# Order of the first work: one chunk's norm first, one cell's weights at the head of the load queue, small products among the first tiles

## The chip, the cores and the metric

The kernel runs on one core of one Trainium2 chip. The metric is device time in microseconds (us) of one launch, the median of three runs. Five engines work side by side, each through its own instructions in program order: TensorE (PE; its weight loads are shown as PEld), VectorE (DVE), ScalarE (ACT), GpSimd (POOL) and SyncE (SP), which issues most of the DMAs. [...]

## The reference, cut to what matters

There are 3327 nodes with 64 features and one adjacency matrix `adj`, 3327 x 3327 in float32. Four residual layers follow each other; each is `x = x + layer(relu(layernorm(x)))`. Layer 0 is two gated graph cells with a relu behind each:

```
def _ggc(x, adj, W, wih, whh, bih, bhh):
    m = adj @ (x @ W)
    gi = m @ wih.T + bih
    gh = x @ whh.T + bhh
    r = sigmoid(i_r + h_r);  z = sigmoid(i_z + h_z)
    n = tanh(i_n + r * h_n)
    return (1.0 - z) * n + z * x
```

where `i_*` and `h_*` are thirds of `gi` and `gh`. The other layers are a product with weights made from the ranks of each row's nonzeros, three products with the squared adjacency, and two products with tanh. That makes eight products of the adjacency with a 64-wide matrix, one behind the other, called k = 0 to 7 in the kernel. The change concerns what happens before and during k = 0.

## The kernel before, in words

**Tiling.** The nodes are padded to 3328, which is 2 halves (`s`) of 13 blocks of 128. The blocks fall into four chunks, 3, 3, 3 and 4 blocks, and the chunks into two groups: group 0 is chunks 0 and 1, group 1 chunks 2 and 3. A tile of the transposed adjacency is one block of 128 source nodes (26 of them) by the target columns of one group: 768 KB for group 0, 896 KB for group 1. A unit of work `(k, c, t)` (`propagate`, L579, matmuls at L607) multiplies the features of the tile's source block with the tile's columns of chunk c, and adds into a bank of PSUM. At 384 columns in float32 a unit is 4 records of L607 in the trace.

**Stages.** `alone(0, 0, ...)` makes k = 0 for group 0 over all 26 tiles. Then `joint(1, 0, ...)` makes k = 0 for group 1, and, from the same tiles, k = 1, whose sources are the results of k = 0; further joint stages follow in the same manner. Within a stage the sources are taken chunk by chunk, so that the tiles of chunk 0 come first. `sweep=2` means that the last two tiles are used first for chunk 0's columns and then for chunk 1's, so that chunk 0 ends earlier.

**Counting.** Along with k = 0 every tile also counts its nonzeros for a later layer: a mask is made on DVE (L466, two pieces for each tile) and multiplied on PE (L542, 4 records). `lag` says by how many tiles the count follows the product. It also sets how many counts are left behind the stage's last product.

**Queues.** There are 20 buffers for tiles (`NBUF`), of which three are kept back and some hold masks. `run()` writes the load of a tile (L405, on SP) as soon as a buffer is free in program order, up to 44 units ahead; on the chip SP then waits for the buffer's last reader. SP's DMAs are taken in order.

**Tasks.** Everything beside the products is a generator in `tasks`. It writes some instructions and yields a number; `spend` (L374) subtracts an estimated product time of each unit from all these numbers (0.86 us for 512 columns) and continues a generator whose number has run out. So the order in which an engine sees its instructions is fixed when the program is built, by these numbers. What lies between two of a generator's steps is lost above the number: it continues at the next unit's end. `finish(c)` runs a generator to its end at once; `propagate` does it where the features of a chunk (`y[k][cs]`) don't exist yet (L597).

**The beginning.** `before_0(c)` (L931) is the first norm of chunk c, in four pieces: sum, mean and difference (L834 to L836); squares, their sum and scaling (L841 to L843); the power -1/2 on POOL (L845); the multiplication that writes the features (L849). After it, and after a yield of 12 to 21, come the transposes of the features (L791 on PE, L793 on ACT). The list at L1036 continues each chunk three times, so that three pieces of all four chunks are written before anything of the fourth. The first unit then finds no features and finishes chunk 0: L849, and its transposes, ahead of the first product. `more_constants` (L238) clears buffers on POOL, loads the first cell's weights into `stage` (`load_cell(0)`, two DMAs on SP behind the first 17 tiles), spreads them (`unfold_cell`, L162), multiplies W1 into the input gates (`fold_cell`, L175 and L181), and computes the third hidden gate of each chunk (`ahead_of_cell`, L201 and L202), which needs only the norm's transposed features. It does the same for the second cell later, loads more weights, and folds those of layer 2 (`fold_hops`).

**After k = 0.** When the last unit of a chunk is written, `after_0` starts: the sums go from PSUM to SBUF on ACT and DVE (L824, L825), the gates are formed (L876 on PE, L881 on ACT), DVE and ACT combine them (L886 to L908), and the result is transposed back (L774, L944). These are the sources of k = 1.

Of the kernel before, what the change touches and what calls it, by code (L numbers as in the profile page):

```python
# [87 lines left out]
def sources_of(*chunks):  # L88
    return [s * NB + b for c in chunks for s in range(2) for b in range(*CH[c])]


def upper(n):
    return slice(n * D, (n + 1) * D)
# [3 lines left out]
def kernel(  # L97
# [9 lines left out]
    nc = tc.nc  # L107
# [18 lines left out]
    stage = const.tile([P, 7 * D + NBIAS], F32, name="stage")  # L126
# [24 lines left out]
    def load_cell(cell):  # L151
        nc.sync.dma_start(out=stage[upper(0), :7 * D].rearrange("p (w f) -> p w f", f=D),
                          in_=weights[:, (W1, W2)[cell]:(W1, W2)[cell] + 7])
        if cell == 0:
            nc.sync.dma_start(out=stage[upper(0), 7 * D:], in_=bias_cols)

    def unfold_cell(cell):

        n = 3 * D + (NBIAS if cell == 0 else 0)
        i, ps = take()  # L160
        for h in range(2):
            nc.tensor.matmul(ps[upper(h), :n], ident[:, :D], stage[:, 4 * D:4 * D + n], start=True, stop=True)  # L162
        v = ps[:, :3 * D].rearrange("p (g f) -> p g f", f=D)
        for h in range(2):
            nc.vector.tensor_copy(cells[upper(1 - h), cell, h, 0:3], v[upper(1 - h)])
        if cell == 0:
            nc.vector.tensor_copy(bcol, ps[:, 3 * D:n])
        give(i)

    def fold_cell(cell):  # L170

        i, ps = take()
        for n in range(2):
            for h in range(2):
                nc.tensor.matmul(ps[upper(h), upper(n)], stage[:, :D], ident[:, :D], start=True, stop=True)  # L175
        tr = work.tile([P, P], F32, name="t2")
        nc.scalar.copy(tr, ps[:, :P])
        give(i)
        yield 1.0
        i, ps = take()  # L180
        mm(ps[:, :3 * D], tr, stage[:, D:4 * D])  # L181
        v = ps[:, :3 * D].rearrange("p (g f) -> p g f", f=D)
        for h in range(2):
            nc.vector.tensor_copy(cells[upper(h), cell, h, 0:2], v[upper(h), 0:2])
            nc.vector.tensor_copy(cells[upper(h), cell, h, 3], v[upper(h), 2])
        give(i)
# [49 lines left out]
        yield from product(1, 2)  # L236

    def more_constants():  # L238
        nc.gpsimd.memset(stage, 0.0)
        nc.gpsimd.memset(cells, 0.0)  # L240
        for c in range(NC):
            for h in range(2):
                nc.gpsimd.memset(both[c][upper(h), h], 0.0)
        nc.gpsimd.memset(bd, 0.0)
        yield 5.0
        load_cell(0)
        yield 20.0
        unfold_cell(0)
        yield 1.0

        full = work.tile([P, P], BF16, name="t2")
        nc.gpsimd.memset(full, -TWO7)
        nc.gpsimd.affine_select(out=tri, in_=full, pattern=[[-1, P]], compare_op=ALU.is_gt, fill=0.0,
                                base=0, channel_multiplier=1)
        nc.gpsimd.affine_select(out=tri, in_=tri, pattern=[[-1, P]], compare_op=ALU.not_equal, fill=TWO7 * TWO7,
                                base=0, channel_multiplier=1)
        nc.gpsimd.memset(tri[:, P - 1:P], 0.0)
        nc.gpsimd.memset(bitsb, BITS)
        nc.gpsimd.memset(lasty, 0.0)
        wide = work.tile([P, P], F32, name="t2")  # L260
        nc.gpsimd.memset(wide, 0.0)

        for i, (bi, bh) in enumerate(((BI1, BH1), (BI2, BH2))):
            nc.vector.tensor_add(bsum[:, i], bcol[:, bi:bi + 2], bcol[:, bh:bh + 2])

        nc.vector.tensor_scalar(wide[0:D], wide[0:D], bcol[0:D, BL1:BL1 + 1], None, op0=ALU.add)
        yield 3.0
        i, ps = take()
        mm(ps[:, :D], wide, ident[:, :D])
        nc.vector.tensor_copy(brow[:, 3], ps[:, :D])  # L270
        give(i)
        yield 1.0
        yield from fold_cell(0)
        for c in range(NC):
            yield 1.0
            ahead_of_cell(c)
        yield 50.0
        load_cell(1)
        yield 20.0
        unfold_cell(1)  # L280
        yield from fold_cell(1)
        yield 30.0
        for h in range(2):
            nc.sync.dma_start(out=bd[upper(h), :, upper(h)], in_=weights[:, WL1:WL3])
            for i in range(2):
                nc.sync.dma_start(out=w3[upper(h), :, i], in_=weights[:, WL3 + (h + i) % 2:NW:2])
        yield 5.0
        nc.sync.dma_start(
            out=brow[:, 0:3],
            in_=bass.AP(tensor=bias_rows.tensor, offset=bias_rows.offset, ap=[[0, P], [D, 3], [1, D]]),  # L290
        )
        yield 22.0
        yield from fold_hops()
# [5 lines left out]
    def width(c):  # L299
        return blocks(c) * P  # L300

    def mm(out, lhsT, rhs, start=True, stop=True):


        for h in range(2):
            hs = slice(h * D, (h + 1) * D)
            nc.tensor.matmul(out[hs], lhsT[:, hs], rhs, start=start, stop=stop)  # L307
# [8 lines left out]
    def take(sums=False, either=True):  # L316


        either = either and not sums
        pool = idle_sums if sums else idle_temps  # L320
        if either and idle_sums and (not pool or released[idle_sums[0]] < released[pool[0]]):
            pool = idle_sums
        for c in list(tasks):
            if not pool and c not in running:
                advance(c)
        i = pool.popleft()
        return i, banks[i]

    def give(i):
        released[i] = max(released) + 1  # L330
        (idle_sums if i < 4 else idle_temps).append(i)
# [21 lines left out]
    def advance(c):  # L353
        running.add(c)
        try:
            tasks[c][1] = next(tasks[c][0])
        except StopIteration:
            del tasks[c]
        running.discard(c)

    def begin(c, task):
        finish(c)
        tasks[c] = [task, 0.0]
        advance(c)

    def finish(c):
        while c in tasks:
            advance(c)

    def later_task(us, task):  # L370
        yield us
        yield from task
# [185 lines left out]
    def last_sources(g):  # L558

        w = sum(width(c) for c in GROUPS[g])  # L560
        w0 = CH[GROUPS[g][0]][0] * P
        room = Mask(w)
        v = room.view.rearrange("p s w -> p (s w)").bitcast(F32)
        nc.gpsimd.memset(v, 0.0)  # L564
        yield 4.0
        rows = adjT.rearrange("(q p) (s n) -> q p s n", p=P, s=2)
        for s in range(2):
            nc.sync.dma_start(out=v[s * D:s * D + NQ], in_=rows[:, P - 1, s, w0:w0 + w])
        yield 12.0
        nc.vector.tensor_scalar(v, v, 0.0, 129.0 * TWO7, op0=ALU.not_equal, op1=ALU.mult)  # L570
        for c in GROUPS[g]:
            finish(("count", c))
        yield 1.0
        nc.vector.scalar_tensor_tensor(v, totals[g], -TWO7, v, op0=ALU.mult, op1=ALU.add)
        yield 1.5
        nc.scalar.activation(lastw[g], v, AF.Relu, bias=bitsb)
        room.free()
# [61 lines left out]
    def alone(g, k, sweep, lag=None, parts=False):  # L639
        tiles = [Tile(q, g, KIND[k] == SQUARED) for q in sources_of(*range(NC))]  # L640
        counting = Counting(g, lag)
        chunks = (GROUPS[g][0], *PARTS) if parts else GROUPS[g]
        for t in tiles[:NQ - sweep]:
            for c in chunks:
                put(k, c, t)
            if lag is not None:
                counting.add(t)
        for c in chunks:
            for t in tiles[NQ - sweep:]:
                put(k, c, t)  # L650
                if lag is not None and c == GROUPS[g][0]:
                    counting.add(t)
        counting.rest()
# [277 lines left out]
    def before_0(c):  # L931
        h = nodes(c)
        yield from layernorm_relu(h, c)
        y[0][c] = h
        yield 12.0 + 3.0 * c
        transpose_to_features(h, c)

    def after_0(c, acc):
# [84 lines left out]
    after[:] = [after_0, after_1, after_2, after_3, after_4, after_5, after_6, after_7]  # L1023


    alone(0, 0, sweep=2, lag=5)
    joint(1, 0, sweep=6, later=4, keep=3, lag=2)
    joint(0, 1, sweep=4, later=20, keep=0)
    joint(1, 2, sweep=6, later=6, keep=1)
# [3 lines left out]
    joint(1, 6, sweep=8, later=4, keep=4)  # L1033
    alone(0, 7, sweep=6, parts=True)

    for c in (0, 0, 1, 0, 1, 2, 1, 2, 3, 2, 3, 3):  # L1036
        if c in tasks:
            advance(c)
        else:
            begin(c, before_0(c))  # L1040
    begin(NC, more_constants())
    begin(NC + 1, later_task(130.0, last_sources(0)))
    begin(NC + 2, later_task(155.0, last_sources(1)))
    run()
# [41 lines left out]
```

## Time and profile before

| | us |
|---|---|
| median of 3 runs | 706.61 |
| lowest and highest | 705.86, 706.64 |
| span of the profiled execution, first to last instruction | 703.7 |
| PE busy in the span | 679.8 |
| first instruction of PE | 14.92 |
| first product (L607) | 16.26 |
| last product of chunk 0 in `alone(0, 0)`, last tile | 61.00 |
| last product of chunk 1 in it | 65.41 |
| steady part of `joint(1, 0)` begins | 80.31 |

The profile gives the span and no other time of the profiled execution. The median is 2.9 us longer than that span, which holds what lies around the instructions and the difference between two executions. A row of the timeline gives start, duration from the first start to the last end of merged instructions, engine, line, operation, operands, their number, and in brackets the idle time ahead of it with what ended it. "Idle" on an engine counts only where that engine is what the others wait for.

### The profile page before, as it was taken

To read this page: it belongs to the slowest core of one execution; us is meant where nothing else is said; L and a number is where in the kernel's file an instruction comes from. 1 tells how busy PE (TensorE), PEld (TensorE's weight loads), DVE (VectorE), ACT (ScalarE), POOL (GpSimd) and SP (SyncE) were. 2 spreads that over 40 slices of the span, in tenths; PEclk is the share of its full clock that TensorE was granted. 3 is DMA by queue.
4 is the path that set the end of the run, shared out by engine and by line. 5 is a ranking of instruction groups with operands and counts; after the bars stand their busy time and mean duration, and the time that the engine had idled before them with its cause. 6 is when DMAs were issued, how large, how long until landed. Compare 5 with 4: busy or idle time off the path is not lost.

```text
span 703.7 us, 12628 instructions
## 1 busy us (share of the span) xinstructions
PE 679.8 (97%) x5100; PEld 372.9 (53%) x5100; DVE 350.1 (50%) x746; ACT 271.8 (39%) x422; POOL 80.0 (11%) x114
## 2 busy tenths in 40 slices
PE   1999999999999999999999999999999999999997
PEld 1454666643556787677444444333344444344586
DVE  7556835643997889847523105425271565005101
ACT  1014100122146888888998206832166600000101
POOL 4300000002284233111100000000000000000000
PEclk9999999999999999999999999999999999999999
DMA  9999996089686952683799649973998399927991
GB/s 344 401 385 404 406 405 241 2 314 398 209 279 253 371 177 76 246 297 96 265 390 343 245 151 409 405 276 100 398 366 271 107 391 406 406 81 276 402 403 45
DMA packets 68549, 201.31 MB, mean 286 GB/s; under 512 B 7228, under 2 KB 8228, under 8 KB 68492
## 3 DMA queue, kind: packets, MB, share of 16 engines
q1 hardware_dynamic: 65596, 199.46, 75.9%
q8 instruction: 40, 0.66, 0.4%
q10 hardware_dynamic: 720, 0.85, 0.3%
q0 software_dynamic: 2176, 0.20, 0.2%
q14 instruction: 17, 0.14, 0.1%
HBM read 199.45 MB, written 0.85 MB: 285 GB/s over the span
## 4 chain that ended last, share of the span: by engine, by line
PE 91%; DVE 7%; issue 0%; ACT 0%; DMA 0%; POOL 0%; ACTq 0%; DVEq 0%; POOLq 0%
PE sum L607 77%; PE temp L307 5%; PE temp L542 2%; PE temp L876 2%; PE sum L307 1%; DVE adj L466 1%; PE temp L774 1%; PE sum L876 1%; DVE e L521 1%; DVE st L842 1%; DVE adj L901 1%; DVE t L836 1%; DVE y L841 0%; DVE st L834 0%; DMA xs<-in_x 0%
## 5 line engine op out<-in xcount | busy, mean ns | idle before, releaser
L607 PE MATMUL sum<-adj,y 128*64 128x384 f32 (+3 forms) x3016 | 534.5, 502 | 0.7 <-DVE y L849 0.6
L607 PEld LDWEIGHTS sum<-adj,y 128*64 128x64 f32 x3016 | 243.5, 137 | 237.3 <-issue 212.4
L440 ACT ACTIVATE adj<-adj 128x768 f32<-128x768 f32 (+1 forms) x176 | 144.2, 893 | 45.8 <-PE sum L607 21.9
L466 DVE TENSOR_SCALAR adj<-adj 128x768 bf16<-128x768 f32 (+3 forms) x208 | 114.0, 597 | 39.8 <-PE temp L542 31.8
L824 ACT COPY both<-sum 64x384 f32<-64x384 f32 (+3 forms) x17 | 8.1, 478 | 192.6 <-PE sum L607 191.4
L607 PE MATMUL sum<-e,both 128*64 128x384 bf16 (+1 forms) x624 | 78.5, 339 | 0.5 <-DVE e L521 0.5
L523 ACT ACTIVATE e<-temp,bitsb 128x384 int16<-128x384 f32 (+1 forms) x117 | 66.0, 605 | 15.1 <-PE temp L307 9.9
L825 DVE COPY both<-sum 64x384 f32<-64x384 f32 (+3 forms) x17 | 9.6, 569 | 110.5 <-ACT both L824 110.5
L307 PE MATMUL temp<-adj,tri 128*64 128x384 bf16 (+1 forms) x332 | 56.8, 341 | 0.5 <-DVE e L521 0.2
L442 DVE TENSOR_TENSOR adj<-adj 128x768 f32<-128x768 f32 (+1 forms) x32 | 30.6, 1005 | 52.1 <-DMA adj<-in_adjT 33.4
L845 POOL TENSOR_TENSOR st<-st,mhalf 128x6 f32<-128x6 f32 (+1 forms) x16 | 24.0, 1498 | 283.2 <-DVE st L843 279.5
L607 PEld LDWEIGHTS <-both 128*64 128x64 bf16 x624 | 46.6, 110 | 15.5 <-issue 2.2
L307 PEld LDWEIGHTS <-tri 128*64 128x64 bf16 x416 | 33.5, 110 | 15.3 <-issue 7.1
L521 DVE TENSOR_SCALAR e<-temp 128x384 int16<-128x384 f32 (+1 forms) x49 | 30.1, 617 | 21.1 <-ACT e L523 10.5
L471 POOL DMA_DIRECT2D adj<-totals x52 | 31.5, 607 | 51.2 <-PE temp L307 40.9
L803 DVE STREAM_TRANSPOSE both<-y 32x96 f32<-32x96 f32 (+1 forms) x128 | 35.6, 278 | 2.9
L542 PE MATMUL temp<-adj,behind 128*64 128x384 bf16 x208 | 30.3, 339 | 0.9 <-DVE adj L466 0.7
L819 DVE STREAM_TRANSPOSE y<-t 32x96 f32<-32x96 f32 (+1 forms) x64 | 17.8, 278 | 24.9 <-ACT t L810 24.0
L542 PEld LDWEIGHTS <-behind 128*64 128x64 bf16 x208 | 17.0, 110 | 17.6 <-issue 15.9
L755 DVE COPY t<-sum 128x384 f32<-128x384 f32 x6 | 3.3, 555 | 35.3 <-PE sum L607 35.3
L564 POOL MEMSET adj<- 128x768 f32 (+1 forms) x2 | 1.9, 950 | 145.3 <-PE sum L607 145.3
L523 ACT ACTIVATE e<-sum,bitsb 128x384 int16<-128x384 f32 (+1 forms) x28 | 16.6, 598 | 2.5 <-PE sum L307 2.1
(132 smaller groups left out, 327.8 us busy)
## 6 DMA issues: line engine op xcount, KB each, us to landing
adj<-in_adjT SPq DMA_DIRECT2D x130, 768.0 KB, 8.5
adj<-in_adjT SPq DMA_DIRECT2D x104, 896.0 KB, 12.3
xs<-in_x SPq DMA_DIRECT2D x1, 640.0 KB
adj<-totals POOLq DMA_DIRECT2D x26, 3.0 KB, 5.1
adj<-totals POOLq DMA_DIRECT2D x26, 3.5 KB, 3.0
out<-xs ACTq DMA_DIRECT2D x2, 192.0 KB
out<-xs ACTq DMA_DIRECT2D x1, 256.0 KB
stage<-in_weights SPq DMA_DIRECT2D x2, 112.0 KB, 13.1
```

The source lines that it names most:

```text
L307: nc.tensor.matmul(out[hs], lhsT[:, hs], rhs, start=start, stop=stop)
L440: nc.scalar.activation(sq, v, AF.Square)
L442: nc.vector.tensor_tensor(sq, v, v, ALU.mult)
L466: nc.vector.tensor_scalar(t.mask.view[:rows, half], t.view()[:rows, half], 0.0, None, op0=ALU.not_equal)
L471: nc.gpsimd.dma_start(out=t.mask.view[P - 1:P], in_=totals[t.g][t.q:t.q + D + 1:D, :])
L521: nc.vector.tensor_scalar(wide[:, s], ps[:, :w], BITS, 0.0, op0=ALU.add, op1=ALU.max)
L523: nc.scalar.activation(wide[:, s], ps[:, :w], AF.Relu, bias=bitsb)
L542: nc.tensor.matmul(counts[c][1][s * D:(s + 1) * D, :w], behind[:, NQ - 1 - t.q:NQ - 1 - t.q + D], t.mask.view[:, s, t.cols(c)], start=firs ...
L607: nc.tensor.matmul(acc[h][1][h * D:(h + 1) * D, :w], yq[h], rhs[h], start=first and n == 0, stop=last and n == len(terms) - 1)
L803: nc.vector.transpose(to[at:at + 32, :, q], h[q * 32:(q + 1) * 32, :, s, f * 32:(f + 1) * 32])
L845: nc.gpsimd.tensor_tensor(st[:, 3, :n], st[:, 2, :n], mhalf[:, :n], ALU.pow)
L876: nc.tensor.matmul(ps[upper(1 - s), :w], cells[:, cell, s, g, :], both[c][:, s], start=True, stop=True)
```

## The change

The cleared `stage` and the first cell's two loads are written ahead of everything else of the tasks, so that SP has them ahead of the first tile. Chunk 0's norm is written to its end, with two thirds of chunk 1's beside it; chunks 2 and 3 begin among the first units. The transposes of a chunk come 2.5 after its norm rather than 12 to 21. The first cell's spreading comes after 4.5 rather than 25, so the folding and the third gates move forward too, with 4 rather than 1 between the four gates. The second cell's load and what follows it is counted from there, with 47 rather than 50. The count of k = 0 in group 0 follows the product by 3 tiles rather than 5.

```diff
     def more_constants():
-        nc.gpsimd.memset(stage, 0.0)
         nc.gpsimd.memset(cells, 0.0)
...
         nc.gpsimd.memset(bd, 0.0)
-        yield 5.0
-        load_cell(0)
-        yield 20.0
+        yield 4.5
         unfold_cell(0)
         yield 1.0
...
         give(i)
-        yield 1.0
+        yield 1.5
         yield from fold_cell(0)
         for c in range(NC):
-            yield 1.0
+            yield 4.0
             ahead_of_cell(c)
-        yield 50.0
+        yield 47.0
         load_cell(1)
...
         yield from layernorm_relu(h, c)
         y[0][c] = h
-        yield 12.0 + 3.0 * c
+        yield 2.5
         transpose_to_features(h, c)
...
-    alone(0, 0, sweep=2, lag=5)
+    alone(0, 0, sweep=2, lag=3)
...
-    for c in (0, 0, 1, 0, 1, 2, 1, 2, 3, 2, 3, 3):
+    nc.gpsimd.memset(stage, 0.0)
+    load_cell(0)
+    for c in (0, 0, 0, 1, 0, 1, 1):
         if c in tasks:
             advance(c)
         else:
             begin(c, before_0(c))
     begin(NC, more_constants())
+    begin(2, later_task(4.0, before_0(2)))
+    begin(3, later_task(10.0, before_0(3)))
     begin(NC + 1, later_task(130.0, last_sources(0)))
```

## The prediction

> **What bounds the kernel now.** I read the page's busy times first, then TensorE's (PE's) waits by stretch, the timeline of the beginning, the loads' landings, and the timeline where the first stage ends.
>
> ```profile
> PE 679.8 (97%) x5100; PEld 372.9 (53%) x5100; DVE 350.1 (50%) x746; ACT 271.8 (39%) x422; POOL 80.0 (11%) x114
> ```
>
> 703.7 - 679.8 leaves PE 24 us without work. The waits of PE from 0 to 20 us and from 60 to 82 us:
>
> ```profile
> PE temp L791 <- DVE y L849: 14.9, 1, 14.9
> ...
> PE temp L542 <- DVE adj L466: 0.7, 2, 0.5
> ```
>
> So 14.9 us lie ahead of its first instruction. From 20 to 60 and from 82 to 165 there are no waits; the rest of the span shows under 4 us in all. Whatever PE gains early and doesn't give back is therefore a gain of the whole. The timeline of the beginning (start, duration):
>
> ```profile
> 1.75 24.40 SPq L405 DMA_DIRECT2D adj<-in_adjT  x17
> 5.86 0.55 DVE L834 TENSOR_REDUCE st<-xs 128x6 f32<-128x384 f32 x1
> 6.04 1.34 POOL L845 TENSOR_TENSOR st<-st,mhalf 128x6 f32<-128x6 f32 x1 [4.07 <-DVE st L843]
> ...
> 14.31 1.49 DVE L849 SCALAR_TENSOR_TENSOR y<-t,st 128x384 f32<-128x384 f32 x3
> 14.92 1.55 PE L791 MATMUL temp<-ident,y 128*64 128x128 f32 x12 [14.92 <-DVE y L849]
> 16.26 9.41 PE L607 MATMUL sum<-adj,y 128*64 128x384 f32 x48
> ```
>
> Chunk 0's power is done at 7.38, but its multiplication stands on DVE behind the other chunks' norms until 14.31. The second limit is seen only in the landings. Two loads, each asked alone:
>
> ```profile
> L405 SPq DMA_DIRECT2D adj<-in_adjT x1: 602/602/602, 2.4 to 2.4; - x1
> DMA to landing us min/median/max: 7.4/7.4/7.4
> ...
> L405 SPq DMA_DIRECT2D adj<-in_adjT x1: 1721/1721/1721, 45.6 to 45.6; - x1
> DMA to landing us min/median/max: 15.3/15.3/15.3
> ```
>
> The first is the second tile (t1): it lands at 9.8. The other is the 27th issue, the first tile of group 1: it lands at 60.9, the next at 63.1 (47.4 + 15.7). Group 1's tiles thus come 2.2 to 2.3 apart (896 KB at about 400 GB/s), and group 0's last tile, t25, landed at about 60.9 - 2.25 = 58.65. In between the tiles land 1.95 apart. The windows show DMA full (share 1.00 to 1.05, 400 GB/s) from 4 to 112 us. And PE uses that last tile at 61.00:
>
> ```profile
> 61.00 0.81 PE L607 MATMUL sum<-adj,y 128*64 128x384 f32 x4
> 61.64 0.49 PE L542 MATMUL temp<-adj,behind 128*64 128x384 bf16 x4
> 61.97 1.02 PE L201 MATMUL sum<-both,cells 128*64 128x512 f32 x4
> ```
>
> So PE starts 7 us behind the stream and is only 2.35 us behind it when the stage ends. A start 6 us earlier runs into the loads.
>
> **What the skill says.** "DMA: Bandwidth & Descriptors", Queues, rings and completion order: each of the 16 DMA engines consumes a ring's descriptors in ring order. So loads written first on SP are paid by every tile behind. The trace agrees in order (9.8, 25.5, 31.4, 45.0, 60.9). Its Specifications give a ceiling of 435 GB/s; the trace's 400 to 409 is near it, so an earlier PE brings no faster loads. "TensorE: Matmul & The Clock Gate", Part 1: PE runs at half rate for its first 3.4 us or so of work. Here weight loads come 0.64 apart until 19.3 and 0.32 later: 4.4 us at half rate, a loss of 2.4 (x48 should take 7.74 rather than 9.41, and the transposes 0.82 rather than 1.55). That loss stays, wherever PE starts.
>
> **The change part by part.**
>
> *Norm order.* Chunk 0's L849 now stands behind chunk 1's L834 to L836 only (end about 7.2), so the power's end at 7.38 decides: + 0.05, + 0.55 for L849, + 0.1 to PE = 8.1. The transposes no longer stand ahead of the first product. Chunks 2 and 3 need the same 3.1 to 3.9 us of DVE each, now between masks; DVE stood idle for 5.6 us ahead of 26.03 and, but for short pieces, half of each 4 us up to 44 (2.06 busy). Their features are used from tile 12 (landing 31.4) and 18 (45.0). Hidden.
>
> *Weights ahead of the stream.* SP waits for the clearing of stage: POOL is free at 1.98, + 0.48 (L239's row) = 2.5; then two issues of 0.6 (the rows show 0.61 and 0.60 where the ring isn't full, 1.72 where it was) = 3.75 for tile 0 rather than 1.75. The 832 KB of x keep DMA busy until about 4.7 (299 GB/s from 2 to 4, 377 from 4 to 6), and the weights follow; first bytes come about 1.3 after an issue. So the hole is 0 to 0.5; I take 0.3. The weights cost 0.3 in bytes, and the window that held them before, 36 to 40, moved 336 rather than 400 GB/s, 0.64 more. That 0.94 is paid before t0 now, before t17 till now: t0 lands at 7.85 + 0.94 + 0.3 = 9.1, but t25 only 0.3 later, at 58.95. If SP were slow (1.72 each), 1.5 later; if no hole, 58.65.
>
> *PE up to the last tile.* Before: 61.00 - 14.92 = 46.1 of unbroken work. Added ahead of it: chunk 3's third gate 0.86, and two counts of 0.33, since lag 3 leaves three behind rather than five. 46.1 + 0.86 + 0.66 = 47.6; from 9.1 this gives 56.7, which is 2.2 ahead of t25. So the load decides: about 59.0, against 61.00. Gain 2.0. PE has 2.2 to spare, and this covers the moved transposes (0.66 to 0.87 each), the spreading (0.34), the folding (0.67) and the other gates: all of them counted in 46.1, moved between tiles that come 1.95 apart and take 1.61 (8 records 1.29, count 0.33).
>
> *Behind the last tile.* From 61.00 to 80.31 were 19.3. Gone: the gate 0.86, two counts 0.66. Of PE's 0.73 of waits for masks half should go: DVE was without a pause from 66.8 to 81.3, and with lag 3 the masks of the last two tiles (4 pieces of 0.55) come ahead of it; PE also comes 0.66 earlier: - 0.35. New: chunk 0's gates need L824 and L825 (0.3 + 0.47 + 0.03 + 0.56 = 1.36 after the last product), and count and product in between are 0.98, without the 0.86: + 0.4. Sum 19.3 - 0.86 - 0.66 - 0.35 + 0.4 = 17.85; 59.0 + 17.85 = 76.8 against 80.3. Gain 3.5.
>
> *POOL.* The clearing (0.95 + 5.17 + 0.53) and constants (2.2) now run from about 10.8 to 19.7, with the powers of chunks 2 and 3 behind; the spreading's copies need `cells` at about 18 (cleared at 11.8), the gates need `both` from about 26. Hidden by at least 6.
>
> *Buffers.* The third gates hold two half buffers some 30 us longer: one tile, 1.95 us of lead. SP ran 12.6 us ahead of landing where it was shortest in this stage. Nothing.
>
> *Later.* The yields up to the second cell's load sum to 74 rather than 85, so this load, its spreading (DVE 1.7 us, from 149.56) and the seven small loads (4.6 us of SP from 188.68) and the folding at 223 come 11 to 14 us earlier in the order. SP issued the second weights at 104.89, they landed at 116.2 and were used at 146.95; now about 132: still covered. The copies move from chunk 3's gates to chunk 2's; PE waits for nothing there. Without that cover 1.7; I take 0, with 0.5 to either side. From 112 us on DMA has holes (4 GB/s from 116 to 120) because buffers are full, so PE's shift passes on.
>
> The span goes from 703.7 to 700.2; the median lies 2.9 above the span, as in before: 706.6 - 3.5 = 703.1 us. A change within 0.2% (1.4 us) can't be told from none.
>
> **Rivals.**
>
> *The early start is kept whole.* If the stream has more slack than I read (the landing of t25 is from its neighbours), PE gains 14.92 - 9.1 = 5.8, plus little behind: about 700.6. For it: PE is 97% busy. Against: 58.65 and full DMA.
>
> *The stream begins late.* If the two loads cost what the ring-full issue did, or the 52-byte rows of the biases stall engines, t25 slips by 2.1 to 4.9 and eats the gain: 705.2 to 708.0, say 706. For it: 336 GB/s where they ran. Against: that dip was 0.64.
>
> *Slower.* The clearing of stage stands behind the norm's powers on POOL. SP would wait until about 11.3, tile 0 would be issued at 12.5, 8.8 us past the 3.75 above; then 703.1 + 8.8 = 712. It decides from a delay of 4.9 on, a first tile issued after 8.7. Against: the clearing is written ahead of the norms, and POOL has a pause from 1.98 to 6.04.
>
> *DVE holds the gates.* If the DVE chain behind chunk 1's last product doesn't shorten and new waits replace the 1.2 counted, the gain is the 2.0 of the load: 704.5. This is the upper end of my likeliest case, not a case apart.
>
> **How the numbers follow.** Load-bound gain 0.70, with its own range 702.0 to 704.6 (t25 between 58.65 and 59.5, the part behind between 0 and 2.2, later 0.5); whole start 0.08; late stream 0.14; slower 0.08. The range 701.0 to 705.3 takes the first, half of the second and a little of the third, 0.8. Faster: 0.70 + 0.08 + 0.01 = 0.79; same 0.13; slower 0.08.
>
> **What would show it.** The first product at about 9, without transposes ahead. PE's waits for adj loads, none till now, about 2 us in all, in the last third of the stage. The last tile's chunk-0 product at 58.7 to 59.5. No wait above 0.5 behind it beyond those for L825 and masks; steady products from about 76.8. A first tile issued after 5, or t25 later than 60, makes the prediction wrong on the slow side; a t25 used before 58 on the fast side.

## The result and the profile after

| | before | after |
|---|---|---|
| median, us (20 runs each) | 706.60 | 707.08 |
| lowest and highest | 705.50, 707.44 | 705.30, 709.48 |
| span of the profiled execution | 703.7 | 705.0 |
| first product of PE | 16.26 | 9.18 |
| last product of chunk 0, last tile (t25) | 61.00 | 58.92 |

The ratio of after to before is 1.0005, with a 95% interval of 0.9998 to 1.0012: no difference that can be measured. The likeliest forecast, 703.1, and the whole range, 701.0 to 705.3, lie below it. Lines in the changed kernel are three lower (L607 is now L604, L466 is L463, L307 is L304, L849 is L846).

The page's busy times of after:

```profile
PE 681.6 (97%) x5100; PEld 375.3 (53%) x5100; DVE 349.6 (50%) x746; ACT 272.1 (39%) x422; POOL 75.2 (11%) x114
```

PE's work is the same in number and is busy 1.8 us longer. Now its waits by stretch: the first line is from 0 to 20 us, the next two from 20 to 60, the fourth from 60 to 82, the last from 165 to 240 (total, times, longest):

```profile
PE sum L604 <- DVE st L839: 9.2, 1, 9.2
PE temp L539 <- DVE adj L463: 1.3, 3, 0.7
PE sum L604 <- DMA adj<-in_adjT: 0.3, 1, 0.3
...
PE temp L539 <- DVE adj L463: 1.4, 3, 1.0
...
PE sum L604 <- DVE brow L232: 2.8, 1, 2.8
```

The 14.9 ahead of the first instruction has become 9.2. (The row names L839; what PE needs is L846 below, written 7.52 to 8.08, and the first tile.) The last line is new: before has no wait for L232 anywhere. The beginning in the timeline of after (start, duration):

```profile
2.42 0.57 SPq L152 DMA_DIRECT2D stage<-in_weights  x1
3.04 0.59 SPq L155 DMA_DIRECT2D stage<-in_bias_cols  x1
...
3.67 11.65 SPq L402 DMA_DIRECT2D adj<-in_adjT  x11
...
7.52 0.56 DVE L846 SCALAR_TENSOR_TENSOR y<-t,st 128x384 f32<-128x384 f32 x1 [0.21 <-POOL st L842]
...
9.18 4.62 PE L604 MATMUL sum<-adj,y 128*64 128x384 f32 x16 [9.18 <-DVE st L839]
```

The first tile is issued at 3.67 and the features stand at 8.08; PE starts 1.1 later, with the tile: at the same place e1's trace, below, names the load, at 8.99. The end of the first stage:

```profile
58.92 0.87 PE L604 MATMUL sum<-adj,y 128*64 128x384 f32 x4 [0.27 <-DMA adj<-in_adjT]
```

The start and the use of the last tile came about as forecast. To find where the gain went, I followed one thing through both traces: the start of ACT's copy that takes a chunk's sums from PSUM (L821, before L824), and further on a power of a norm on POOL (L842, before L845). The table gives after's time less before's, in us, in one trace of each; the first row is where before has the event. Traces taken from one and the same order of instructions already differ by 0.5 (e8 below, up to 212 us), so smaller shifts mean nothing.

| | 66.3 | 172.1 | 212.4 | 235.2 | 278.3 | end |
|---|---|---|---|---|---|---|
| after | -2.5 | -3.7 | +2.2 | +1.0 | +0.9 | +1.4 |

The gain of 3.7 us is there at 172 us and gone, with 2.2 more, at 212. In between lies the new wait. PE there, in the timeline:

```profile
199.12 0.82 PE L224 MATMUL temp<-ident,brow 128*64 128x128 f32 x12
...
201.31 0.34 PE L304 MATMUL sum<-bd,t 128*64 128x64 f32 x4
...
206.79 0.68 PE L604 MATMUL sum<-e,both 128*64 128x384 bf16 x6 [2.82 <-DVE brow L232]
...
208.17 2.82 PE L604 MATMUL sum<-adj,y 128*64 128x384 f32 x8
```

And DVE:

```profile
202.73 3.88 DVE L463 TENSOR_SCALAR adj<-adj 127x768 bf16<-127x768 f32 x5
206.53 0.20 DVE L232 COPY brow<-sum 128x64 f32<-128x64 f32 x1
```

L224 is the beginning of `fold_hops`, the folding of layer 2's weights. Its next product, at 201.31, is written to `sum`: `take()` lends whichever bank of PSUM was released longest ago, and here that is one of the four banks in which the products of the adjacency accumulate. The next user of this bank is the product at 206.79. It has to wait until L232, a copy of 0.2 us, has emptied the bank; and this copy stands on DVE behind five mask pieces. In the kernel before, the same two steps stood elsewhere:

```profile
225.20 0.28 PE L307 MATMUL temp<-bd,t 128*64 128x64 f32 x2
...
226.58 0.22 DVE L232 COPY brow<-temp 128x64 f32<-128x64 f32 x1
```

There the folding began at 222.9, its product went to a `temp` bank, no mask pieces stood ahead of the copy, and nobody waited for it. After the wait PE is slow too. The windows of after (us, busy time and count of PE, PEld, DVE, ACT, POOL, granted clock, DMA share, GB/s):

```profile
204.00:206.00 2.00, 0.00 (x0) 0.00 (x0) 2.00 (x3) 0.90 (x2) 2.00 (x4) 1.00 0.90 286
206.00:208.00 2.00, 1.21 (x14) 1.07 (x15) 2.00 (x6) 0.17 (x1) 2.00 (x4) 0.86 0.53 166
208.00:210.00 2.00, 2.00 (x10) 1.00 (x8) 2.00 (x5) 1.15 (x3) 1.56 (x3) 0.50 0.05 12
210.00:212.00 2.00, 2.00 (x18) 1.33 (x16) 0.56 (x2) 0.00 (x0) 1.26 (x3) 0.79 0.03 5
```

The granted clock falls to 0.50: 2 x (0.14 + 0.50 + 0.21) = 1.7 us of PE's time are lost by this estimate, and the eight records of L604 at 208.17 take 2.82 us. The 20 executions agree with it: the five with a mean granted clock of 1.000 took 705.30 to 705.85, the fifteen with 0.996 to 0.998 took 706.73 or more, and their medians differ by 1.6. "TensorE: Matmul & The Clock Gate" in the Trainium skill, Part 1, says that PE drops to half rate after an idle window of about 3.4 us and needs about as long of work to come back. The trace agrees in kind, but here a pause of 2.8, shorter than that window, was enough.

### The profile page after: what moved, and what is told of

Its sections match the earlier page's. It is cut to its first block, busy times and chain, and to the rows that moved or that the text cites. A ratio compares the mean times of both kernels' runs of the same rounds, so it can differ in the third digit from the quotient of the medians.

```text
span 705.0 us, 12613 instructions
## 1 busy us (share of the span) xinstructions
PE 681.6 (97%) x5100; PEld 375.3 (53%) x5100; DVE 349.6 (50%) x746; ACT 272.1 (39%) x422; POOL 75.2 (11%) x114
## 2 busy tenths in 40 slices
DMA packets 68549, 201.31 MB, mean 286 GB/s; under 512 B 7228, under 2 KB 8228, under 8 KB 68492
## 4 chain that ended last, share of the span: by engine, by line
PE 57%; DVE 1%; ACT 0%; POOL 0%; issue 0%; ACTq 0%; DVEq 0%; POOLq 0%
PE sum L604 54%; PE temp L304 3%; PE temp L771 1%; POOL st L842 0%; DVE xs L1016 0%; ACT t L1013 0%; DVE both L822 0%; ACT both L821 0%; DVE e L518 0%; ACTq L1018 0%; PE sum L304 0%; DVE y L846 0%; DVE y L838 0%; DVE t L833 0%; DVE st L831 0%
## 5 line engine op out<-in xcount | busy, mean ns | idle before, releaser
L604 PE MATMUL sum<-adj,y 128*64 128x384 f32 (+3 forms) x3016 | 538.1, 503 | 10.4 <-DVE st L839 9.2
L604 PEld LDWEIGHTS sum<-adj,y 128*64 128x64 f32 x3016 | 246.9, 138 | 244.3 <-issue 208.2
L463 DVE TENSOR_SCALAR adj<-adj 128x768 bf16<-128x768 f32 (+3 forms) x208 | 114.3, 598 | 32.7 <-PE temp L539 24.7
L604 PE MATMUL sum<-e,both 128*64 128x384 bf16 (+1 forms) x624 | 73.5, 340 | 3.4 <-DVE brow L232 2.8
L821 ACT COPY both<-sum 64x384 f32<-64x384 f32 (+3 forms) x17 | 8.1, 478 | 154.0 <-PE sum L604 152.9
L842 POOL TENSOR_TENSOR st<-st,mhalf 128x6 f32<-128x6 f32 (+1 forms) x16 | 24.8, 1553 | 298.2 <-DVE st L840 298.2
L604 PEld LDWEIGHTS <-both 128*64 128x64 bf16 x624 | 41.0, 110 | 22.1 <-issue 9.8
L304 PE MATMUL temp<-adj,tri 128*64 128x384 bf16 (+1 forms) x332 | 51.4, 344 | 1.3 <-DVE e L518 1.2
L518 DVE TENSOR_SCALAR e<-temp 128x384 int16<-128x384 f32 (+1 forms) x46 | 28.3, 616 | 20.8 <-ACT e L520 10.9
L304 PEld LDWEIGHTS <-tri 128*64 128x64 bf16 x416 | 28.5, 110 | 17.3 <-issue 9.5
L539 PE MATMUL temp<-adj,behind 128*64 128x384 bf16 x208 | 34.1, 340 | 2.8 <-DVE adj L463 2.8
L539 PEld LDWEIGHTS <-behind 128*64 128x64 bf16 x208 | 21.0, 110 | 15.9 <-issue 11.7
L304 PE MATMUL sum<-adj,tri 128*64 128x384 bf16 (+1 forms) x84 | 15.8, 335 | 0.8 <-DVE e L518 0.7
```

The source lines that it names most:

```text
L463: nc.vector.tensor_scalar(t.mask.view[:rows, half], t.view()[:rows, half], 0.0, None, op0=ALU.not_equal)
L518: nc.vector.tensor_scalar(wide[:, s], ps[:, :w], BITS, 0.0, op0=ALU.add, op1=ALU.max)
L539: nc.tensor.matmul(counts[c][1][s * D:(s + 1) * D, :w], behind[:, NQ - 1 - t.q:NQ - 1 - t.q + D], t.mask.view[:, s, t.cols(c)], start=firs ...
L604: nc.tensor.matmul(acc[h][1][h * D:(h + 1) * D, :w], yq[h], rhs[h], start=first and n == 0, stop=last and n == len(terms) - 1)
L842: nc.gpsimd.tensor_tensor(st[:, 3, :n], st[:, 2, :n], mhalf[:, :n], ALU.pow)
```

## The experiments

The theories, by the letters that the expectations use. **A**: the early folding costs it, by a borrowed bank whose copy stands behind masks on DVE. **B**: the earlier second cell or the other things that moved with it cost it. **C**: the early start is worth nothing in the end, whatever else happens. **D**: the dense stage k = 2 swallows about 2 us of any head start by itself. Times are medians, with before's on the same chip; shifts are against before's trace, as in the table above. That one trace is of an execution about 1 us faster than its median (shown further down), so a shift behind 219 us and a median can differ by as much.

### The folding later, in the changed kernel

```diff
 # e1_fold_late: the wait ahead of fold_hops, L289
-        yield 22.0
+        yield 33.0
```

> The changed kernel, with only the folding of layer 2's weights put back by 11 (its yield 33 for 22); the second cell's load and spreading and the last loads stay early. Theory A (the changed kernel gains about 3.6 us up to 199 us of the span and loses about 5 between 199 and 232, because the folding's small product stands in a PSUM bank that the next accumulators of k = 2 need, and its copy on VectorE, L232, is queued behind mask pieces; PE waits 2.8 and then runs slowly for some us): the wait for L232 is gone, the time is 706.6 - 3.6 = 703.0, within 0.7. Theory B (the earlier second cell, with its load and its copies, costs the gain): nothing comes back, about 707. Theory C (an early start is worth nothing, since the later stages are tied to loads): about 707 though the wait is gone.

704.34 (before 706.33), ratio 0.9972 (0.9961 to 0.9983). The wait for L232 is gone. The shift stands at -3.4 at 212 us and falls to -1.6 only behind it, where the folding now stands ahead of chunk 1's sums. One number ahead of `fold_hops` returns about 2.5 us of after's time, each taken against before on its own chip. Theory A had forecast 703.0 within 0.7, so 1.3 are missing: the place of the folding counts, and not only that it is early.

### Everything from the second cell on later

```diff
 # e2_all_late: L274
-        yield 47.0
+        yield 58.0
```

> The changed kernel with yield 58 for 47: the second cell, the last loads and the folding all stand where they did before. Theory A: 703.0 as in the run with the folding alone put back, within 0.7. Theory B: 703.0 here, but 707 there. Theory C: about 707 in both.

705.20 (706.33), ratio 0.9982 (0.9976 to 0.9989). The second cell's spreading (L162) begins at 139.88, where after had it at 124.07, and the products of k = 1 now wait for the features of the next chunk, 131 to 200 us:

```profile
PE sum L604 <- DVE y L941: 1.6, 1, 1.6
```

The shift falls from -3.8 to -2.0 there. So in the changed kernel the earlier second cell saves 1.6 to 1.8 at this point and costs nothing: B falls. By the medians of e1 and e2 0.9 of it is left. Both A and B had forecast 703.0 here and missed by 2.2; neither had this wait in it. (The folding, later too, makes the whole faster than after all the same.)

### Another bank for the same product

```diff
 # e3_temp_bank: fold_hops, L230
-        i, ps = take()
+        i, ps = take(either=False)
```

> The changed kernel with the folding where the change has it, but its second product takes a bank of the other four, not one that accumulators use next. If the bank ties PE to L232 (theory A), the wait of 2.8 us is gone or under 1 us and the time is 703 to 705. If the work itself in this crowded place costs the time, whatever bank it uses, about 707.

705.00 (706.33), ratio 0.9985 (0.9977 to 0.9992). The order of the instructions is after's; only the bank differs. The wait shrinks and is that of a later use of the `temp` bank:

```profile
PE temp L304 <- DVE brow L232: 0.7, 1, 0.7
```

In this trace the clock stays at 1.00, and the shift at 212 is -1.2 rather than +2.2. But the trace is of an execution of 703.62, 1.4 below the median. Six of the 17 executions, with a mean clock of 0.996 or 0.997, took 706.11 to 706.55, and no trace shows how long PE waited in them. So the bank is part of the cause; how large a part in most executions is open.

### The second cell, the last loads and the folding early, in the kernel before

```diff
 # e4_before_fold_early: L277
-        yield 50.0
+        yield 36.0
```

> The kernel before with yield 36 for 50, nothing else: the second cell, the last loads and the folding move forward to where the changed kernel has them (the folding's product again in one of the four accumulator banks). Theory A: the same wait of 2 to 3 us for L232 near 205, and a time about 4 to 5 us above before, 710.5 to 711.6. Theories B and C: B also says slower by 4 to 5, but without the wait; C says the same as before, 706.6.

710.46 (706.33), ratio 1.0056 (1.0042 to 1.0070): 4.1 us slower, without the new start. The edit moves the second cell and the last loads along with the folding, but up to the folding nothing is lost: the shift is -0.3 at 172 us and at 195. At 212 it is +5.4. PE's wait there, and the two windows from its end on:

```profile
PE sum L607 <- DVE brow L232: 2.9, 1, 2.9
```

```profile
210.00:212.00 2.00, 1.73 (x14) 1.43 (x15) 2.00 (x7) 0.10 (x1) 1.77 (x3) 0.50 0.35 97
212.00:214.00 2.00, 2.00 (x12) 1.08 (x10) 2.00 (x5) 1.22 (x3) 1.20 (x2) 0.70 0.01 2
```

The same wait and the same half clock. A holds.

### The folding behind k = 2, with the change and without

```diff
 # e5_fold_after_k2: after, L289
-        yield 22.0
+        yield 140.0
 # e8_before_fold_after_k2: before, L292
-        yield 22.0
+        yield 129.0
```

> The changed kernel with the folding's yield 140 for 22: it comes behind the last mask product of k = 2, where VectorE and ScalarE have little to do. Putting it back by 11 gave 704.3 and a shift against before of 3.8 us at 168 us of the span that shrank to 1.6 by 340. Theory A (what was lost between 200 and 340 is lost to the folding's own instructions among the crowded ones of k = 2): the shift stays above 3, time 702.8 to 703.5. Theory D (k = 2 itself, where VectorE and ScalarE are as full as PE, swallows about 2 us of any earlier start): 704.3 to 705 again.

> The kernel before with the folding's yield 129 for 22, which puts it behind the mask products of k = 2, nothing else. Theory A: the folding's PE work is 1.3 us anywhere, but among the crowded instructions it costs more; 0 to 1 us faster than before. Theory D: the same as before within 0.5. The difference between this kernel and the changed one with the folding in the same place is what the change at the start is worth by itself: 3 to 3.6 by theory A, 1.5 to 2 by theory D.

With the folding out of k = 2 in both, the changed kernel takes 703.36 (before 706.32; ratio 0.9956, 0.9944 to 0.9969) and the unchanged one 707.46 (706.32; 1.0014, 1.0008 to 1.0021). All else of the change is thus worth 707.46 - 703.36 = 4.1 us, above the 3 to 3.6 that theory A had forecast: C falls. For D, e5 has to be held against e8, since before has the folding inside k = 2 and these two don't. e5 lies 3.1 ahead of e8 at 172 us, 2.4 at 212 (0.5 is a wait for a load there) and 2.9 at 235: the dense stage keeps 0.2, not 2. D falls as well. e8 itself had been forecast 0 to 1 faster than before and is 1.1 slower: in the kernel before, the folding is cheaper within k = 2 than behind it. In the changed kernel the two places cost the same (e9 below, 703.36 too).

### The last tile: five counts behind rather than three

```diff
 # e6_fold_after_k2_lag5: e5, and
-    alone(0, 0, sweep=2, lag=3)
+    alone(0, 0, sweep=2, lag=5)
```

> As the run with the folding behind k = 2, but with a lag of 5 tiles for the count, as before the change. PE's three waits for masks in the first stage (1.3 us) should go. If the loads set the stage's end (prediction), the last tile's chunk-0 product stays at 58.7 to 59.3 and PE waits 1 to 2 us for loads instead; two more counts then stand behind it, and the time is 0.3 to 1 us above the run with lag 3. If PE and its masks set the end, this product comes at about 57.5 and the time is no worse than with lag 3.

704.50 (706.32), ratio 0.9970 (0.9959 to 0.9981), 1.1 slower than e5, where 0.3 to 1 had been forecast. PE's use of t25 in e6:

```profile
59.83 0.87 PE L604 MATMUL sum<-adj,y 128*64 128x384 f32 x4 [1.87 <-DMA adj<-in_adjT]
```

With two counts fewer ahead of it PE arrives earlier and stands 1.87 us before the load. That is the limit that the prediction named. The tile comes 0.8 to 0.9 later than in e5 (59.02) or after (58.92), with the same queue ahead of it and DMA just as full (402 GB/s from 40 to 60). The profiled execution took 705.43, the longest of the seven and 0.9 above their median, so this may be chance of the one execution; it isn't settled.

### The norms' order and the transposes alone

```diff
 # e7_norm_order_only: before, and
-        yield 12.0 + 3.0 * c
+        yield 2.5
...
-    for c in (0, 0, 1, 0, 1, 2, 1, 2, 3, 2, 3, 3):
+    for c in (0, 0, 0, 1, 0, 1, 1):
...
+    begin(2, later_task(4.0, before_0(2)))
+    begin(3, later_task(10.0, before_0(3)))
```

> The kernel before with only the order of the norms and the earlier transposes of the change (weights, third gates, lag and all later yields as before). The first product starts at 8 to 8.5. Load limit: the last tile's chunk-0 product comes at 58.7 to 59.0, 2.0 to 2.3 ahead of before, whatever PE gained at the start; the third gates still stand behind, so the shift at the end of the stage is 2.0 to 2.5 rather than the 3.6 of the whole change. Time by theory A, with the folding where it was: 704.3 to 705; by theory D: 706 or more. If the loads don't limit: 701.

704.97 (706.32), ratio 0.9980 (0.9969 to 0.9990). PE starts at 8.11, a whole us earlier than in after, and waits for loads on the way to t25:

```profile
PE sum L607 <- DMA adj<-in_adjT: 2.2, 7, 0.6
```

Of 14.92 - 8.11 = 6.8 us of an earlier start 1.5 are left at the end of the stage, where 2.0 to 2.5 had been forecast. Its t25 is used at 59.50 and not at 59.0 or before, and PE doesn't wait for it: three of the third gates (L201, about 0.65 each) stand among the last tiles, so PE itself comes later than the load. By the medians 1.35 arrive. In the trace the shift is -1.4 until 212 us and -0.5 from 219 on; e8 loses 1.1 in the same place (from -0.5 to +0.6), though it has before's instructions in before's order up to there. Both show a wait of L876 for L825 there, 0.5 and 0.7, which before's one profiled execution doesn't have.

### The old place, and one link after another

```diff
 # e9_fold_at_old_unit: after, L289, puts the folding at the unit where before has it
-        yield 22.0
+        yield 36.0
 # e10_clearing_later: after, the task that begins with clearing a buffer on GpSimd (L561) moves
-    begin(NC + 2, later_task(155.0, last_sources(1)))
+    begin(NC + 2, later_task(163.0, last_sources(1)))
 # e11_copy_on_scalar: after, L232
-        nc.vector.tensor_copy(brow[:, 0], ps[:, :D])
+        nc.scalar.copy(brow[:, 0], ps[:, :D])
 # e12_both: the edits of e9 and e10 together
```

> The changed kernel with the folding's yield 36 for 22: its first product stands at the same place among PE's instructions as in the kernel before (behind chunk 1's gates of k = 1, where before hid it best). The start's gain of 3.6 should now be passed on but for what the crowded k = 2 takes: 703.0 to 704.0, at or below the run with the folding behind k = 2 (703.4). If k = 2 swallows the gain wherever the folding stands, 704.5 or more.

> The changed kernel, its folding untouched, with last_sources(1) begun at 163 rather than 155, so that GpSimd's clearing of 128x896 comes two descriptor writes later. In the changed kernel the mask piece ahead of L232 took 1.96 us beside this clearing, against 0.55 for the others. If the clearing makes it slow, the piece is 0.55, PE's wait for L232 1.4 rather than 2.8, its clock stays full, and the time falls by 2 to 3.5, to 703.5 to 705. If the queue of pieces alone makes the wait, nothing changes: 707.

> The changed kernel with the one copy L232 on ScalarE rather than VectorE, behind five instructions there; bank and place stay. If the wait comes from VectorE's queue of mask pieces, it is under 0.5 us, PE's clock stays full and the time is 703.5 to 705. If the bank is late for another reason, the wait stays at 2 to 3 and the time at 707.

> The changed kernel with both: the folding at its old place (36 for 22) and the clearing later (163 for 155). By the sum of the two readings it is the fastest here, 702.5 to 703.5. If the slow mask piece of k = 2 was hidden once the folding is away, it is the same as the run with the folding at its old place alone.

| | median (before 706.90) | ratio, interval | shift at 172 | 212 | 235 | end |
|---|---|---|---|---|---|---|
| e9 | 703.36 | 0.9952, 0.9940 to 0.9965 | -3.7 | -2.8 | -2.4 | -2.5 |
| e10 | 703.92 | 0.9961, 0.9948 to 0.9973 | -3.5 | -0.7 | -3.2 | -1.9 |
| e11 | 702.83 | 0.9946, 0.9933 to 0.9958 | -3.5 | -2.3 | -3.4 | -3.0 |
| e12 | 703.10 | 0.9950, 0.9936 to 0.9963 | -3.6 | -3.6 | -3.7 | -2.9 |

e9 is the change with the folding where it was: faster by 3.5. Of the 0.9 by which its shift falls from 172 to 212, 0.7 is a wait for a load. e10 takes away one of the masks' delays. In after the last of the five pieces takes 1957 ns where the two ahead of it take 545 and 593, while GpSimd clears a buffer:

```profile
L463 DVE TENSOR_SCALAR adj<-adj x3: 545/593/1957, 203.7 to 204.7; 127x768 bf16<-127x768 f32 x3
...
205.33 0.86 POOL L561 MEMSET adj<- 128x896 f32 x1
```

With the clearing elsewhere, DVE shows:

```profile
202.92 2.49 DVE L463 TENSOR_SCALAR adj<-adj 127x768 bf16<-127x768 f32 x5
205.33 0.20 DVE L232 COPY brow<-sum 128x64 f32<-128x64 f32 x1
```

Five pieces in 2.49 rather than 3.88. The wait for L232 halves, to 1.4, and the clock doesn't drop at all:

```profile
206.00:208.00 2.00, 2.00 (x22) 1.33 (x20) 2.00 (x6) 1.22 (x3) 1.85 (x2) 1.00 0.07 22
```

"SBUF — State Buffer", Who interferes with whom, says that a `tensor_scalar` in a mode that uses two ports and a GpSimd instruction exclude each other from a shared pair of ports, and that the second to come is held for the whole of the first. The piece is slow beside the clearing and not without it, which agrees. But it loses 1.4 us beside a clearing of 0.86, more than one such hold gives, and the trace shows neither the mode nor who held the ports first. So that the clearing slows the piece is shown, and how isn't.

e11 leaves the place, the bank, the masks and the slow piece as they are, and moves the one copy to ACT:

```profile
203.21 0.23 ACT L232 COPY brow<-sum 128x64 f32<-128x64 f32 x1
...
203.99 0.66 PE L604 MATMUL sum<-e,both 128*64 128x384 bf16 x6
...
205.02 1.46 PE L604 MATMUL sum<-adj,y 128*64 128x384 f32 x8
```

The product that waited until 206.79 runs at 203.99, and the next eight records take 1.46 rather than 2.82. This version has the lowest median of all, 4.1 us below before and also below its forecast of 703.5 to 705. e12 had been forecast to be the fastest and isn't. e10 and e12, in which the whole task behind L561 comes later, lose 0.9 of their shift between 239 and 271 us, and e9 and e11 don't; why isn't settled.

The loss can now be summed. e11 and after have PE's work in the same order. From 172 to 212 e11's shift goes from -3.5 to -2.3: 1.2, the folding's own work, come earlier than in before, and what the dense stage takes. After's goes from -3.7 to +2.2: 5.9. The difference of 4.7 is the wait, 2.8, and the clock, 1.7, to within 0.2. By the medians it is 707.08 - 702.83 = 4.25, where a quarter of after's executions don't have the drop of the clock.

## Why the prediction was wrong

**Norm order and first product: right.** Forecast about 9, found 9.18, without transposes ahead.

**Weights ahead of the stream: right.** SP issued the two loads at 2.42 and 3.04 and the first tile at 3.67 (2.5 and 3.75 forecast). The two issues took 0.57 and 0.59; that a full ring is what makes others take 1.72, as the prediction has it, no run here shows. DMA's share from 4 to 8 us was 0.90, a hole of 0.4 (0.3 forecast). The rival of a late stream and the slower rival of a late clearing fell here.

**PE up to the last tile: the load's time was right, the slack wasn't.** t25 was used at 58.92, forecast 59.0. But PE was to stand 2.2 ahead of it with about 2 us of waits for loads; after shows 0.3. From 9.18 PE took 49.7 rather than 47.6, 1.3 of it in waits for masks: with `lag=3` a count comes two tiles sooner behind its mask (e6, with `lag=5`, shows 0.4), and the sum had priced the counts and not their masks. Nothing was lost by it, since the load came then anyway. e6 and e7, with 1.9 and 2.2 of waits for loads, show that the loads are the limit as soon as PE is faster; the rival of a whole early start fell with them.

**Behind the last tile: the gain was right, its inside not.** I let half of 0.73 us of waits for masks go; they grew to 1.4. The same tile pattern in the middle of the next stage, eight records that before has at 112.65, comes at 109.06: -3.6, forecast 3.5. At 172 us it is still -3.7.

**Later: this step failed.** It said that the folding comes 11 to 14 us earlier in the order, took 0 with 0.5 to either side, and let PE's shift pass on. The folding came 23.8 us earlier (L224 from 222.92 to 199.12), of which 3.7 are PE's shift, so about 20 in the order. It was priced as so much PE work under cover, with the loads, the spreading and the folding in one sentence. What it lacked were three questions on one product: which bank it takes, which queue empties that bank, and what stands ahead there. The answers, an accumulator's bank, DVE, and five mask pieces, cost 2.8 of wait and 1.7 of clock. e4 shows the same wait and clock without the new start, and e3, e10 and e11 take one link each away (e3 in one trace only). None of the rivals had this mechanism, and the range stopped below the result because this step's bounds of 0.5 were a guess and not the worst that the queue could do.

**The second cell in the same step: right that it costs nothing, without the reason it is needed.** Its earlier copies were to cost 0. e2 shows that without them the changed kernel waits 1.6 there.

**The median from the span.** I put the median 2.9 above the span, from before alone. All 13 profiled executions with both times lie 1.9 to 2.2 above (after 707.09 with 705.0, e4 710.07 with 708.2), and so do before's own later executions, 1.8 to 2.1. So before's trace is of an execution about 1 us faster than its median, and the shifts in the tables behind 219 us understate gains by as much: e11's is -3.0 at the end and 4.1 by the medians, and e7 and e8 lose about this much between 212 and 219 where before's trace lacks a wait. That this is the whole of the difference isn't shown.

The forecast of 703.1 stands within 0.3 of e9 and e11, but not for the kernel it was made for.

## What to carry to other kernels

In this kernel a step that moved in the program's order cost not its work but what waited for it. So ask of every product which bank it takes, who empties it, and what stands in that queue ahead. The queue that a small copy stands in can matter more than its length: here 0.2 us on ACT rather than DVE was worth 4.2 us. When a gain is seen early in the trace and not in the time, follow one event through both traces; the stretch where the difference jumps is where to look.

## What was unexpected of the hardware

Pauses of PE of 2.8 and 2.9 us (after, e4) took the granted clock to 0.50; in the traces of e6, e2, e10 and e3 pauses of 1.9, 1.6, 1.4 and 0.7 left it at 1.00. The drop added 1.7 to a pause of 2.8, and five of after's 20 executions show a mean clock of 1.000, so it doesn't come every time. A mask piece of 0.55 us took 1.96 while GpSimd cleared a buffer for 0.86. At the start of the kernel PE was slow, 16 records of L604 in 4.62 us, while the granted clock was shown as 1.00; at 196.54 after's 16 records take 2.75.
